# A vision tower's first attention: the order of its block steps inside a chunk, how its results are added, and the tokenizer's first steps

## Chip, cores and metric

The kernel runs on one core of a Trainium2 chip. The metric is device time in microseconds (us). The kernel before the change takes 2812.41 us, the median of three runs (2807.48 to 2813.47).

The core has five engines with a queue of instructions each, worked off in the order of issue: TensorE (PE; PEld are its weight loads), VectorE (DVE), ScalarE (ACT), GpSimd (POOL) and SyncE (SP, which issues DMAs). They meet through semaphores. SBUF is the core's working memory, PSUM the small memory into which TensorE writes.

## What is computed

128 images of 128x128 pass a tokenizer (two convolutions with batch norms, 64 tokens of 256 features an image), then two layers of attention and feed-forward. The change is in the tokenizer and in the first attention, which is this, over 64 tokens of an image, with 8 groups of 32 features:

```python
Q = x @ Wq.T; K = x @ Wk.T; V = x @ Wv.T          # x: layer norm of h
diff = Q.reshape(B, L, 1, G, Dg) - K.reshape(B, 1, L, G, Dg)
attn = einsum('bqkgd,d->bqkg', relu(diff), w_mlp) + b_mlp[0]
attn = softmax(relu(attn), axis=2)
out = einsum('bqkg,bkdg->bqdg', attn, V.reshape(B, L, Dg, G))
h = h + out.reshape(B, L, d_att)
```

The costly part is relu(q - k) for each query, key, image and feature. It is also max(q, k) - k, and the kernel uses both forms.

## The kernel before

All in float32; the running state h stays in SBUF as the tile `h2`, 128 partitions (2 images x 64 tokens) x 64 pairs of images x 256 features. The functions are called one after another: tokenizer, relu_attention, expert_attention, linear_attention, route, experts. The order of the work in the first two is written out by hand (`manual_schedule`): an engine's queue holds its instructions in the order in which the Python code issues them.

**Tokenizer** (L58 to L264). The image rows are loaded in 16 tiles `xt` of 512 KB, three in flight (`load`, L80); the first three, and all later ones, are issued by SP, the small weights `w1bd`, `bnv1`, `w`, `bnv2` by ACT's queue. `conv1(r)` (L123) is two matmuls, ACT writes one half (`ev`, L135), DVE the other (`h`, L132), and `differences(r)` (L139) makes two more on DVE. `between` (L146) makes `v`, on ACT, POOL or DVE. Five such rows precede the main loop, in which a `Unit` makes 72 matmuls (`products`, L177). In the preamble, at r == 2, stand the weights' negation (ACT, L229), the sum `w02` (POOL, L230) and the second batch norm's factors (`scale_offset`, L104 to L111: four small DVE instructions around a power on POOL, L108, and L233).

**First attention** (L267 to L719). 8 blocks of 16 images; a block has 8 chunks of 8 queries, so there are 64 chunks. A chunk makes 32 tiles of 128 x 8 queries x 64 keys, one for each pair of images' place i (0 to 15) and half of the features hf (0, 1), in three ways: `larger` (DVE, L486, max(q, k), four at a time straight from the queries in PSUM), `difference` (POOL subtracts, L494, ACT takes relu, L495, two at a time) and `by_query` (ACT, L504, four instructions for half a tile). `add(i0, hf)` sums four of them over the features with TensorE (`summed`, L301) into the scores `sc`, which `begin` (L481) has started with a correction `kb` for the max form. For the chunk before (`old`), `less_max` (DVE: L520, L521, L522), `exponents` (ACT, L527), `sums` (DVE, L530, L531), `weights` (POOL, L534), `transpose` (PE, L543) and `transposed` (ACT, L551) follow inside the current chunk. `queries` (PE, L422) and `queried` (ACT, L433) prepare the next one.

Between these, a table of work puts the steps of the neighbouring blocks at named places of a chunk: `at(n, place, step)` files a step under chunk n, and `do(n, place)` runs it there. Places O, A, B, C hold ACT's copies and normalisations; X, Y, Z hold PE's transposes, key, value and outcome products; V1 and V2 hold DVE's steps, W one of POOL's. In the order of PE's queue a chunk is: add(0,0), X, add(8,0), add(4,0), queries, Y, add(8,1), add(0,1), add(4,1), begin, transpose of the old, add(12,0), Z, add(12,1). For DVE: larger(0,0), larger(4,0), less_max, V1, larger(0,1), sums, larger(4,1), larger(12,1), V2. For ACT: relu of difference(8,0), O, half a by_query, relu of (10,0), exponents, half a by_query, relu of (8,1), A, relu of (10,1), queried, B, half a by_query, relu of (12,0), half a by_query, relu of (14,0), transposed, C.

A block's results come from `outcome` (PE, L443; two halves of the features), four copies `outcome_copied` (ACT, L454), transposes `back` (PE, L459) and `added` (DVE, L468), which adds 512 values a partition to `h2`. A result of half the features belongs to four of every eight neighbouring features, so `added` reads and writes `h2` with the feature index d outside in memory steps of 8 values (32 bytes). The PSUM tiles of all block steps come from one pool of three (`apq`). `first` (L565) prepares the first block ahead of the first chunk: statistics, normalisation, transposes, keys of both halves, queries, the correction.

## Time and profile before

| what | us |
|---|---|
| median of three runs | 2812.41 |
| the profiled execution | 2801.97 |
| its span, first to last instruction | 2800.3 |
| tokenizer, 0 to 180.7 | 180.7 |
| first attention up to its first search for a maximum, 180.7 to 218.1 | 37.4 |
| the chunks, 218.1 to 1118.2 | 900.1 |
| eight chunks of one block in the middle, 433.43 to 548.83 | 115.40 |

In those eight chunks the engines are busy so long: PE 112.86 us, DVE 106.13, ACT 99.84, POOL 100.12. The granted clock of TensorE is 1.00 throughout the chunks (0.97 over the tokenizer).

A row of the timeline gives the start, the length, the engine, the line, the operation, the tiles (written <- read), the shape, the count of instructions merged into the row, and in brackets the engine's idle time ahead of it and whose end stopped it. PE's rows overlap by the latency of the last matmul: 16 records of `summed` take 1.92 us, 24 take 2.78, so that one `add`, eight records, occupies PE for 0.86.

### The profile page before, as it was taken

The numbers are of one execution on the slowest core, as the hardware profiler recorded it, in microseconds if no ns is written. First come the engines' busy times: TensorE is split into PE (matmuls) and PEld (weight loads), VectorE is DVE, ScalarE is ACT, GpSimd is POOL, SyncE is SP. The second block draws the span as 40 slices with busy tenths as digits, with TensorE's granted clock in tenths as the row PEclk, the third lists the DMA queues.
The fourth block names the chain that finished last, engine by engine and source line by source line (L and its number), as shares of the span: only waits on it lengthen the run. The fifth ranks groups of instructions, "written<-read, shape, count | busy, mean of one in ns | idle before, by whom it ended". The sixth has DMA issues, their size and how long they took to land.

```text
span 2800.3 us, 76977 instructions
## 1 busy us (share of the span) xinstructions
PE 2608.5 (93%) x33260; PEld 1750.3 (63%) x33260; DVE 2041.6 (73%) x3046; ACT 1611.9 (58%) x3348; POOL 1633.1 (58%) x1412
## 2 busy tenths in 40 slices
PE   7989999999999998799999999999899964999997
PEld 3554444444444443688888888887466644888886
DVE  6759899998999998577778777776467766344443
ACT  3228888888888887456666566665354430233332
POOL 3328988888888888666565665643133211454444
PEclk9999999999999999799999999999899975999998
DMA  3000000000000000000000000000444432455554
GB/s 106 31 12 1 2 1 2 1 2 2 1 2 1 2 2 2 12 11 18 11 18 11 11 18 11 18 11 15 116 91 110 97 87 105 163 194 193 194 195 132
DMA packets 138064, 140.81 MB, mean 50 GB/s; under 512 B 107923, under 2 KB 121509, under 8 KB 130032
## 3 DMA queue, kind: packets, MB, share of 16 engines
q1 hardware_dynamic: 126640, 118.40, 14.1%
q0 software_dynamic: 7648, 14.77, 1.6%
q8 instruction: 263, 4.31, 0.6%
q10 hardware_dynamic: 3424, 2.60, 0.3%
q14 instruction: 89, 0.73, 0.1%
HBM read 103.93 MB, written 32.54 MB: 49 GB/s over the span
## 4 chain that ended last, share of the span: by engine, by line
PE 81%; DVE 10%; ACT 3%; issue 3%; POOL 1%; DMA 1%; ACTq 0%; SPq 0%; DVEq 0%; POOLq 0%
PE sc L301 13%; PE ph L1714 6%; PE po L1730 6%; PE pqk L894 6%; PE pv L906 5%; PE pz L975 5%; PE pc L177 4%; PE pt L962 4%; PE sc L926 4%; DVE m L486 3%; PE pq L1174 3%; PE po L989 2%; PE pt L543 2%; PE sc L481 2%; PE pv L387 2%
## 5 line engine op out<-in xcount | busy, mean ns | idle before, releaser
L494 POOL TENSOR_TENSOR m<-q,k 128x1024 f32<-128x1024 f32 x384 | 719.7, 1905 | 34.0 <-PE sc L301 11.5
L486 DVE TENSOR_TENSOR m<-pc,k 128x2048 f32<-128x2048 f32 (+1 forms) x320 | 643.7, 2058 | 0.0
L301 PE MATMUL sc<-m,wide 128*32 128x512 f32 x4096 | 533.8, 599 | 23.5 <-DVE m L486 17.7
L495 ACT ACTIVATE m<-m 128x1024 f32<-128x1024 f32 x384 | 402.1, 1049 | 17.1 <-POOL m L494 17.1
L301 PEld LDWEIGHTS sc<-m,wide 128*32 128x32 f32 x4096 | 128.1, 109 | 272.0 <-issue 132.8
L504 ACT ACTIVATE m<-k,q 128x64 f32<-128x64 f32 x1024 | 270.3, 337 | 0.9 <-DVE k L380 0.9
L938 DVE TENSOR_REDUCE mx<-sc 128x16 f32<-128x1024 f32 x128 | 156.1, 1220 | 155.0 <-PE sc L926 129.8
L953 POOL TENSOR_TENSOR e<-e,mx 128x1024 f32<-128x1024 f32 x128 | 243.7, 1904 | 10.1 <-POOL mx L952 0.2
L898 ACT COPY qk<-pqk 128x512 f32<-128x512 f32 x256 | 138.8, 604 | 132.6 <-PE pqk L894 132.6
L952 POOL TENSOR_TENSOR mx<-mx,gate 128x16 f32<-128x16 f32 x128 | 27.8, 217 | 312.8 <-ACT z L983 146.8
L1714 PE MATMUL ph<-xt,w1s 128*128 128x256 f32 x896 | 201.0, 383 | 1.3 <-DVE xt L1705 0.8
L1730 PE MATMUL po<-w2s,hT 128*128 128x256 f32 x896 | 198.0, 379 | 0.0
L965 ACT COPY pT<-pt 128x512 f32<-128x512 f32 x256 | 138.9, 599 | 99.3 <-PE pt L962 98.7
L1714 PEld LDWEIGHTS ph<-xt,w1s 128*128 128x128 f32 x896 | 171.9, 192 | 26.0 <-DVE xt L1705 1.2
L1718 ACT ACTIVATE hT<-ph,w1s 128x256 f32<-128x256 f32 x224 | 93.4, 471 | 155.5 <-PE ph L1714 82.3
L1730 PEld LDWEIGHTS po<-w2s,hT 128*128 128x128 f32 x896 | 168.1, 190 | 21.7
L894 PE MATMUL pqk<-xT,w 64*128 64x128 f32 x2048 | 169.4, 289 | 2.6 <-issue 2.4
L939 DVE TENSOR_TENSOR e<-sc,mx 128x1024 f32<-128x1024 f32 x128 | 156.8, 1225 | 4.4
L1748 POOL DMA_INDIRECT out<-y,rout x56 | 56.8, 1014 | 172.6 <-ACT hT L1718 124.8
L894 PEld LDWEIGHTS pqk<-xT,w 64*128 64x128 f32 x2048 | 142.5, 189 | 20.3 <-issue 11.6
L945 DVE TENSOR_REDUCE mx<-e 128x16 f32<-128x1024 f32 x128 | 153.2, 1197 | 1.2 <-ACT e L942 1.0
L962 PE MATMUL pt<-ident,e 128*128 128x128 f32 x1024 | 144.4, 282 | 4.5 <-POOL e L953 1.2
(292 smaller groups left out, 4974.8 us busy)
## 6 DMA issues: line engine op xcount, KB each, us to landing
w1s<-in_we SPq DMA_DIRECT2D x30, 1028.0 KB
w2s<-in_we SPq DMA_DIRECT2D x30, 1024.0 KB
xt<-in_x SPq DMA_DIRECT2D x16, 512.0 KB
hd<-h SPq DMA_DIRECT2D x16, 512.0 KB
x<-hd SPq DMA_DIRECT2D x16, 512.0 KB
h<-hd SPq DMA_DIRECT2D x4, 2048.0 KB
hx<-h SPq DMA_DIRECT2D x4, 2048.0 KB
out<-h SPq DMA_DIRECT2D x4, 2048.0 KB
```

What stands on the lines that cost most here:

```text
L301: nc.tensor.matmul(dst[j : j + 32], wide[:, hf, s : s + 32], part, start=start, stop=stop)
L486: nc.vector.tensor_tensor(m, bcast(self.pq[:, hf, i : i + n], 3, T), k, ALU.max)
L494: nc.gpsimd.tensor_tensor(m, bcast(self.q[:, hf, s : s + 2], 3, T), k, ALU.subtract)
L495: nc.scalar.activation(m, m, AF.Relu)
L504: nc.scalar.activation(self.parts[i, hf][:, q], self.blk.k[:, hf, i], AF.Relu, bias=self.q[:, hf, i - NB // 2, q : q + 1], scale=-1.0,)
L894: nc.tensor.matmul(pq[par][:, k, eh, :], w[r, f : f + P], self.xT[r, fc], start=True, stop=True)
L938: nc.vector.tensor_reduce(mx, sc, AX.X, ALU.max)
L939: nc.vector.tensor_sub(e, sc, bcast(mx, 2, T))
L953: nc.gpsimd.tensor_mul(e, e, bcast(sm, 2, T))
L962: nc.tensor.transpose(pt[:, cq, :], e[:, i : i + 2, :].rearrange("p e s -> p (e s)"), c.ident)
L1714: nc.tensor.matmul(ph[:, j], self.w1[:, w0 : w0 + P], self.xt[:, fc], start=(fc == 0), stop=(fc == 1))
L1730: nc.tensor.matmul(po, self.hT[:, f, r * P : r * P + P], self.w2[:, f, :], start=(f == 0), stop=(f == 7))
```

## The change

It has five parts.

1. Tokenizer: the small first weights go to SP's queue, ahead of SP's loads; row tile 0 goes to ACT's queue. The weights' negation and the sum `w02` move from r == 2 to r == 1; the second batch norm's factors move from r == 2 to behind the last `between` of the preamble.
2. `first` is cut: the keys of the second half of the features, their copies (both now on DVE), the sums and the correction run inside chunk 0, behind its first difference and its first `larger`; so does `begin` of chunk 0.
3. In a chunk PE's queue becomes: add(0,0), add(8,0), add(4,0), X, queries, add(8,1), add(0,1), add(4,1), begin, transpose of the old, Z, add(12,0), add(12,1). Place Y is gone; Z stands ahead of V2, add(12,0) and `transposed`.
4. The block steps are filed under other chunks and places. Counted 0 to 7 within a block of chunks, PE's steps (for the next block, and for the results of the block before) are now: 0: X and Z, a transpose each; 1: X and Z, one half of the outcome each; 2: Z a transpose; 3: X two `back`, Z a transpose; 4: X two `back`, Z keys; 5: X keys, keys, Z keys; 6: X values, Z key sums and values; 7: X values, values. `added` stands in V1 of chunks 3 and 4 (before: 2 and 3), the statistics of the block after next in V2 of chunks 3 and 4 (before: 4 and 5).
5. `back(i)` transposes both halves of two pairs, and `added(i)` adds 2 pairs x 256 whole features: `h2` is read and written without gaps, the PSUM tile is read in steps of 32 values. It is called four times a block, 512 values a partition each, as before.

```diff
@@ -77,19 +77,19 @@
     ):
         rows = {}
 
-        def load(r):
+        def load(r, eng=nc.sync):
             rows[r] = xt = xp.tile([P, 8, B], F32, tag="xt", name="xt")
-            nc.sync.dma_start(xt, x[r])
+            eng.dma_start(xt, x[r])
 
 
         w1bd = wp.tile([P, P], F32, name="w1bd")
         nc.vector.memset(w1bd, 0.0)
         bnv1 = wp.tile([P, 4], F32, name="bnv1")
         bnv2 = wp.tile([P, 4, 4], F32, name="bnv2")
-        load(0)
         for k in range(2):
-            nc.scalar.dma_start(w1bd[k * 64 : (k + 1) * 64, k * 64 : (k + 1) * 64], w1)
-            nc.scalar.dma_start(bnv1[k * 64 : (k + 1) * 64, :], bn1)
+            nc.sync.dma_start(w1bd[k * 64 : (k + 1) * 64, k * 64 : (k + 1) * 64], w1)
+            nc.sync.dma_start(bnv1[k * 64 : (k + 1) * 64, :], bn1)
+        load(0, nc.scalar)
         for r in range(1, 3):
             load(r)
 
@@ -223,16 +223,16 @@
                     nc.gpsimd.tensor_add(w[:, :, 1], w[:, :, 0], w[:, :, 2])
                 differences(r)
                 if r == 1:
+                    nc.scalar.mul(w[:, :, 2], w[:, :, 2], -1.0)
+                    nc.gpsimd.tensor_add(w02, w[:, 0:2], w[:, 2:4])
                     between(0, 0, 0)
                 elif r == 2:
                     between(0, 0, 1)
-                    nc.scalar.mul(w[:, :, 2], w[:, :, 2], -1.0)
-                    nc.gpsimd.tensor_add(w02, w[:, 0:2], w[:, 2:4])
-                    s2, o2 = scale_offset(lambda i: bnv2[:, i, :], [P, 4], "2")
-                    n2 = wp.tile([P, 4], F32, name="n2")
-                    nc.vector.tensor_scalar_mul(n2, s2, -1.0)
             for k in range(2):
                 between(0, 2, k)
+            s2, o2 = scale_offset(lambda i: bnv2[:, i, :], [P, 4], "2")
+            n2 = wp.tile([P, 4], F32, name="n2")
+            nc.vector.tensor_scalar_mul(n2, s2, -1.0)
             for m in range(4):
                 for ab in range(4):
                     u = Unit(m, ab)
@@ -453,19 +453,22 @@
                     self.oT = np_.tile([P, 2, NP, 2, T], F32, tag="oT", name="oT", bufs=1)
                 nc.scalar.copy(self.oT[:, hf, :, par], self.ps["o", hf][par])
 
-            def back(self, hf, i):
-                self.ps["h", hf, i] = pt = psq.tile([P, 4, P], F32, tag="pq", name="pto")
-                for n in range(4):
-                    nc.tensor.transpose(
-                        pt[:, n], self.oT[:, hf, 4 * i + n].rearrange("p b t -> p (b t)"), c.ident
-                    )
-
-            def added(self, hf, i):
-
-                p0 = self.p0 + 4 * i
-                hv = h2[:, p0 : p0 + 4].rearrange("p n (d g) -> p n g d", g=8)[:, :, hf * 4 : hf * 4 + 4]
-                pt = self.ps.pop(("h", hf, i))
-                nc.vector.tensor_add(hv, hv, pt.rearrange("p n (g d) -> p n g d", d=32))
+            def back(self, i):
+
+                self.ps["h", i] = pt = psq.tile([P, 2, D], F32, tag="pq", name="pto")
+                for n in range(2):
+                    for hf in range(2):
+                        nc.tensor.transpose(
+                            pt[:, n, hf * P : hf * P + P],
+                            self.oT[:, hf, 2 * i + n].rearrange("p b t -> p (b t)"),
+                            c.ident,
+                        )
+
+            def added(self, i):
+
+                hv = h2[:, self.p0 + 2 * i : self.p0 + 2 * i + 2].rearrange("p n (d g) -> p n d g", g=8)
+                pt = self.ps.pop(("h", i))
+                nc.vector.tensor_add(hv, hv, pt.rearrange("p n (g d) -> p n d g", d=32))
 
         class Chunk:
 
@@ -576,9 +579,11 @@
                 x.keyed(s, 0, s == 1)
             x.queries(0)
             x.queried(0)
+
+        def first_rest(x):
             for s in range(2):
                 x.keys(s, 1)
-                x.keyed(s, 1, s == 1)
+                x.keyed(s, 1, True)
             x.key_sums()
             x.correction()
 
@@ -588,60 +593,61 @@
             at(n + 9, "X", of(x.outcome, 0))
             at(n + 9, "A", of(x.outcome_copied, 0, 0))
             at(n + 9, "B", of(x.outcome_copied, 0, 1))
-            at(n + 9, "Y", of(x.outcome, 1))
+            at(n + 9, "Z", of(x.outcome, 1))
             at(n + 9, "C", of(x.outcome_copied, 1, 0))
-            at(n + 9, "Z", of(x.back, 0, 0))
             at(n + 10, "O", of(x.outcome_copied, 1, 1))
-            at(n + 10, "X", of(x.back, 0, 1))
-            at(n + 10, "V1", of(x.added, 0, 0), of(x.added, 0, 1))
-            at(n + 10, "Z", of(x.back, 1, 0))
-            at(n + 11, "X", of(x.back, 1, 1))
-            at(n + 11, "V1", of(x.added, 1, 0), of(x.added, 1, 1))
+            for i in range(4):
+                at(n + 11 + i // 2, "X", of(x.back, i))
+                at(n + 11 + i // 2, "V1", of(x.added, i))
             if b == 0:
-                for i, (m, pe, act) in enumerate(((0, "X", "A"), (1, "X", "A"), (2, "X", "A"), (2, "Y", "B"))):
-                    at(m, pe, of(x.values, i))
-                    at(m, act, of(x.valued, i))
+                for i in range(4):
+                    at(i, "X", of(x.values, i))
+                    at(i, "A", of(x.valued, i))
                 continue
 
             if b == 1:
                 at(0, "V1", of(x.statistics, 0), of(x.statistics, 1))
                 at(0, "W", x.factors)
                 at(0, "C", of(x.normal, 0), of(x.normal, 1))
-                at(1, "A", of(x.normal, 2))
-                at(1, "B", of(x.normal, 3), of(x.normal, 4))
+                at(1, "A", of(x.normal, 2), of(x.normal, 3))
+                at(1, "X", of(x.transpose, 0))
+                at(1, "B", of(x.transposed, 0))
+                at(1, "Z", of(x.transpose, 1))
+                at(1, "C", of(x.normal, 4))
             else:
-                at(n - 12, "V2", of(x.statistics, 0))
-                at(n - 11, "V2", of(x.statistics, 1))
-                at(n - 10, "W", x.factors)
-                at(n - 9, "B", of(x.normal, 0), of(x.normal, 1))
-                at(n - 8, "A", of(x.normal, 2))
-                at(n - 8, "B", of(x.normal, 3), of(x.normal, 4))
-            at(n - 8, "Z", of(x.transpose, 0))
-            at(n - 7, "O", of(x.transposed, 0))
+                at(n - 13, "V2", of(x.statistics, 0))
+                at(n - 12, "V2", of(x.statistics, 1))
+                at(n - 11, "W", x.factors)
+                at(n - 11, "C", of(x.normal, 0))
+                at(n - 10, "B", of(x.normal, 1))
+                at(n - 9, "C", of(x.normal, 2))
+                at(n - 8, "X", of(x.transpose, 0))
+                at(n - 8, "A", of(x.transposed, 0))
+                at(n - 8, "B", of(x.normal, 3))
+                at(n - 8, "Z", of(x.transpose, 1))
+                at(n - 8, "C", of(x.normal, 4))
+            at(n - 7 if b > 1 else n - 6, "O", of(x.transposed, 1))
             at(n - 6, "A", of(x.normal, 5))
-            at(n - 6, "B", of(x.normal, 6), of(x.normal, 7))
-            at(n - 5, "X", of(x.transpose, 1))
-            at(n - 5, "A", of(x.transposed, 1))
-            at(n - 5, "Y", of(x.keys, 0, 0))
-            at(n - 5, "B", of(x.keyed, 0, 0))
-            at(n - 5, "Z", of(x.transpose, 2))
-            at(n - 4, "O", of(x.transposed, 2))
-            at(n - 4, "X", of(x.transpose, 3), of(x.keys, 0, 1))
-            at(n - 4, "A", of(x.transposed, 3))
-            at(n - 4, "B", of(x.keyed, 0, 1))
-            at(n - 4, "Z", of(x.values, 0))
-            at(n - 3, "O", of(x.valued, 0))
-            at(n - 3, "X", of(x.keys, 1, 0))
-            at(n - 3, "A", of(x.keyed, 1, 0))
-            at(n - 3, "Z", of(x.values, 1))
-            at(n - 2, "O", of(x.valued, 1))
-            at(n - 2, "X", of(x.keys, 1, 1))
-            at(n - 2, "A", of(x.keyed, 1, 1))
-            at(n - 2, "Z", x.key_sums)
+            at(n - 6, "Z", of(x.transpose, 2))
+            at(n - 6, "C", of(x.normal, 6))
+            at(n - 5, "O", of(x.transposed, 2))
+            at(n - 5, "A", of(x.normal, 7))
+            at(n - 5, "Z", of(x.transpose, 3))
+            at(n - 4, "O", of(x.transposed, 3))
+            at(n - 4, "Z", of(x.keys, 0, 0))
+            at(n - 4, "C", of(x.keyed, 0, 0))
+            at(n - 3, "X", of(x.keys, 0, 1), of(x.keys, 1, 0))
+            at(n - 3, "A", of(x.keyed, 0, 1))
+            at(n - 3, "B", of(x.keyed, 1, 0))
+            at(n - 3, "Z", of(x.keys, 1, 1))
+            at(n - 2, "O", of(x.keyed, 1, 1))
+            at(n - 2, "X", of(x.values, 0))
+            at(n - 2, "A", of(x.valued, 0))
+            at(n - 2, "Z", x.key_sums, of(x.values, 1))
+            at(n - 2, "C", of(x.valued, 1))
             at(n - 1, "V1", x.correction)
-            at(n - 1, "X", of(x.values, 2))
+            at(n - 1, "X", of(x.values, 2), of(x.values, 3))
             at(n - 1, "A", of(x.valued, 2))
-            at(n - 1, "Y", of(x.values, 3))
             at(n - 1, "B", of(x.valued, 3))
 
         def do(n, place):
@@ -652,29 +658,30 @@
             seq = [(x, q0) for x in blocks for q0 in range(0, T, 8)]
             first(blocks[0])
             ch, old = Chunk(*seq[0]), None
-            ch.begin()
             for n in range(len(seq)):
                 new = None
                 ch.difference(8, 0)
                 ch.larger(mvp, 0, 4, 0)
                 do(n, "O")
+                if n == 0:
+                    first_rest(blocks[0])
+                    ch.begin()
                 ch.by_query(14, 1, 0)
                 ch.add(0, 0)
+                ch.difference(10, 0)
+                ch.larger(mvp, 4, 4, 0)
+                ch.add(8, 0)
+                ch.add(4, 0)
                 do(n, "X")
-                ch.difference(10, 0)
-                ch.add(8, 0)
-                ch.larger(mvp, 4, 4, 0)
-                ch.add(4, 0)
+                if n + 1 < len(seq):
+                    seq[n + 1][0].queries(seq[n + 1][1])
                 if old:
                     old.less_max()
                     old.exponents()
                 ch.by_query(14, 1, 1)
-                if n + 1 < len(seq):
-                    seq[n + 1][0].queries(seq[n + 1][1])
                 ch.difference(8, 1)
                 do(n, "A")
                 do(n, "V1")
-                do(n, "Y")
                 ch.difference(10, 1)
                 if n + 1 < len(seq):
                     seq[n + 1][0].queried(seq[n + 1][1])
@@ -697,6 +704,7 @@
                     new.begin()
                 if old:
                     old.transpose()
+                do(n, "Z")
                 ch.larger(mgp, 12, 2, 1)
                 do(n, "V2")
                 ch.difference(14, 0)
@@ -704,7 +712,6 @@
                     old.transposed()
                 do(n, "C")
                 ch.add(12, 0)
-                do(n, "Z")
                 ch.add(12, 1, True)
                 old, ch = ch, new
             old.less_max()
@@ -714,7 +721,7 @@
             old.transpose()
             old.transposed()
             for n in range(len(seq), len(seq) + 12):
-                for place in ("O", "X", "A", "V1", "Y", "B", "V2", "C", "Z"):
+                for place in ("O", "X", "A", "V1", "B", "Z", "V2", "C"):
                     do(n, place)
         assert not work
 
```

## The prediction

> **What bounds the kernel now.** I read the page first: the busy shares and the chain that ended last.
>
> ```profile
> PE 2608.5 (93%) x33260; PEld 1750.3 (63%) x33260; DVE 2041.6 (73%) x3046; ACT 1611.9 (58%) x3348; POOL 1633.1 (58%) x1412
> ...
> PE 81%; DVE 10%; ACT 3%; issue 3%; POOL 1%; DMA 1%; ACTq 0%; SPq 0%; DVEq 0%; POOLq 0%
> ```
>
> TensorE carries the chain. The change takes no matmul away (16 transposes of results a block before and after), so it can only change how long PE waits. For that I cut one block into its eight chunks, at each chunk's first add:
>
> ```profile
> core 0: us, PE busy (x) PEld busy (x) DVE busy (x) ACT busy (x) POOL busy (x), PEclk, DMA share, GB/s
> 433.43:447.08 13.65, 12.88 (x116) 4.90 (x111) 12.24 (x10) 13.05 (x31) 12.67 (x8) 1.00 0.01 2
> ...
> 461.13:475.99 14.86, 13.54 (x121) 5.16 (x117) 14.28 (x12) 13.39 (x33) 12.01 (x8) 1.00 0.00 1
> ...
> sum 115.40, PE 112.86 PEld 49.30 DVE 106.13 ACT 99.84 POOL 100.12; mean PE 14.11 PEld 6.16 DVE 13.27 ACT 12.48 POOL 12.52
> ```
>
> PE looks full, but a matmul row counts its latency as busy. By starts, a chunk without waits is 8 adds of 0.86, queries 1.05, begin 1.06, transposes 1.08 and 0.4 of switching: 10.45 us. A block adds values 4 x 1.92, keys 4 x 1.85, transposes 8 x 0.6, outcomes 2 x 1.45, key sums 0.85: 23.65. So 8 x 10.45 + 23.65 = 107.25 us, and 8.15 of the 115.40 are waits. Two kinds make them. First ScalarE's, in the timeline of chunk 0:
>
> ```profile
> 430.17 1.15 PE L543 MATMUL pt<-ident,e 128*64 128x64 f32 x32
> ...
> 431.79 0.57 ACT L551 COPY at<-pt 128x512 f32<-128x512 f32 x1
> 432.26 1.06 ACT L495 ACTIVATE m<-m 128x1024 f32<-128x1024 f32 x1
> 433.21 1.06 ACT L504 ACTIVATE m<-k,q 128x64 f32<-128x64 f32 x4
> 434.17 1.04 ACT L495 ACTIVATE m<-m 128x1024 f32<-128x1024 f32 x1
> 435.27 1.91 PE L301 MATMUL sc<-m,wide 128*32 128x512 f32 x12 [0.39 <-ACT m L495]
> ```
>
> Between PE's weight transposes and the second half of add(8,0) ScalarE does four things in order; the add waits. With PE work in place X ahead of it the wait is covered, as in chunks 4 to 6. Second VectorE's, where it adds results (chunk 3):
>
> ```profile
> 360.85 0.70 DVE L520 TENSOR_REDUCE pc<-sc 128x8 f32<-128x512 f32 x1 [0.40 <-PE sc L301]
> 361.54 0.66 PE L459 MATMUL pto<-ident,oT 128*128 128x128 f32 x4
> ...
> 362.46 2.17 DVE L468 TENSOR_TENSOR h<-h,pto 128x512 f32<-128x512 f32 x2
> ...
> 364.55 2.27 DVE L486 TENSOR_TENSOR m<-pc,k 128x2048 f32<-128x2048 f32 x1
> ...
> 369.86 1.07 PE L301 MATMUL sc<-m,wide 128*32 128x512 f32 x8 [0.39 <-DVE m L486]
> ```
>
> The two adds push both following `larger`, and add(4,1) waits. Today they start directly behind less_max (its last instruction, L522, ran from 361.85 to 362.54): their transposes are through.
>
> **Part 1, tokenizer.** PE starts densely at 33.55:
>
> ```profile
> 21.06 3.51 POOL L230 TENSOR_TENSOR w<-w 128x1536 f32<-128x1536 f32 x1 [8.12 <-ACT w L229]
> 21.32 4.86 DVE L154 TENSOR_TENSOR v<-h 128x1536 f32<-128x1536 f32 x1
> ...
> 27.95 0.81 DVE L132 TENSOR_SCALAR h<-pa,s,o 128x512 f32<-128x512 f32 x1
> 28.81 4.81 PE L130 MATMUL pa<-xt,w1bd 128*128 128x512 f32 x6 [4.10 <-DVE h L132]
> 33.55 2.81 PE L177 MATMUL pc<-v,w 128*64 128x256 f32 x24
> ```
>
> DVE's L154 took 1.76 at 34.84; here, beside POOL's sum, 4.86. Moved up, the sum runs from about 16.4 (ACT's negation takes the gap behind its second row, 15.3 to 16.4) to 19.9 and no longer covers L154: -3.1. The factors (26.10 to 27.95) go behind the preamble: -1.85. L132 of row 3 then starts near 23.1, and row 4's matmul follows its twin (24.7); rows 4 and 5 and their copies take to 27 to 29. I take -5.7 at 33.55, bounds -3 (the clock row is half here; it may stay so) and -7. [...] The swapped queues: the second w1bd issue stays at about 2.06 and landed 5.7 later beside three row tiles; now it has one tile and 1 MB of `w` beside it. I take 0, bounds -2 and +1. SP's tiles 1 and 2 are now issued behind four small DMAs of 0.6, some 2 us later, and are wanted at 12.55 and 15.32; that is hidden unless they land 5 us later than today. The factors' new waits (POOL behind one L154, then 1.0) hold DVE to about 34, while PE reaches the next unit only near 37: nothing.
>
> **Part 2, chunk 0.** DVE's first `larger` starts at about 194.9, not 199.6, and two key copies (0.69) come between; so DVE is 2.1 ahead, begin finds no wait (1.07), and chunk 0 ends 2.6 earlier. Bounds -1 and -3.5.
>
> **Part 5, whole rows.** L468 takes 1.12 (median); its nearest row for the new form, L204 (same size, strided PSUM in, SBUF without gaps out), 0.69. I take 0.70 (bounds 0.6 to 1.5): -1.7 of DVE a block. [...]
>
> **Parts 3 and 4, the chunk.** Here X moves behind add(8,0) and add(4,0). Chunk 3, walked from its first add = 0. ScalarE: the weight transposes end 2.4 earlier (Z 0.7, two adds 1.72); then L551 0.5, C 0.55, relu 0.96, O 0.57, by_query 0.96, relu 1.0, i.e. 4.54: the relu ends at 2.15. Add(8,0) ends at 2.15 + 0.06 + 0.86 = 3.07 in place of 1.72: 1.35 lost, no X in front to cover it. Add(4,0) ends at 3.93, the two `back` at 4.6 and 5.15. less_max is done at 1.86, but the first row add waits for its transposes: 4.7 to 5.4, the second to 6.1. Then larger 2.25, sums 0.83, larger 2.25 with latencies: 11.4; add(4,1) ends 0.92 later, at 12.3, where PE alone would be at 8.85: 3.4 lost. Behind add(4,1): begin to transposes 2.25, Z 0.7, two adds 1.72: 17.0 us. DVE still has larger 1.13, the moved statistics 2.1 and two larger 4.4: done at 19.0, so less_max of chunk 4 starts 1.75 late, which its own wait for transposes hides (row adds done at 5.5, chunk 17.6).
>
> So behind a waiting row add stand both other `larger` and the sums on DVE, and for these wait add(0,1), add(4,1) and, through POOL's weights, the next transposes.
>
> The same walk for the other chunks, each with its own steps in C, O, X, A and Z. The second wait that ScalarE makes is at add(8,1): its relu (10,1) ends at about 5.5 (today 5.95 with one step in A, both behind exponents, by_query and relu (8,1)) plus what A holds or waits for. Before, after, and PE's own work after in brackets:
>
> | chunk | before | after | why |
> |---|---|---|---|
> | 0 | 13.65 | 13.6 (11.65) | relu at 2.25: 1.45; add(8,1) 0.5 |
> | 1 | 14.05 | 15.2 (13.35) | relu 2.1 behind C and O: 1.3; A copies an outcome that X makes late: 0.55 |
> | 2 | 14.86 | 14.2 (11.05) | `transposed` waits for the second outcome in Z, relu at 2.9: 2.1; add(8,1) 1.05 |
> | 3 | 14.89 | 17.0 (12.25) | above |
> | 4 | 14.87 | 17.6 (13.5) | relu 1.55: 0.75; row adds 3.35 |
> | 5 | 14.66 | 17.0 (16.0) | C copies keys that Z ends late, relu 1.8: 1.0 |
> | 6 | 13.84 | 15.7 (15.15) | A copies values that X makes late: 0.55 |
> | 7 | 14.58 | 15.15 (14.3) | C copies values, relu 1.8: 0.85 |
>
> Sum 115.4 before, 125.4 after: waits of 18.2 in place of 8.15, +10 a block (bounds: +2, rival a, and +13, with 0.4 more at each relu). POOL's (10,0) ends before the chunk's start in most chunks today and stays covered; if not, relu waits for it as long.
>
> **The sum.** Six full blocks +60. Block 0 (no results yet, chunks 1 to 7): relu waits of 0.9 to 1.7 a chunk, +5.5. Block 7 (no next block): chunks 3 and 4 wait as above, 1.6 + 3.7, chunk 1 +1.2, chunk 2 -1.8: +4.7. Chunk 0 -2.6, tokenizer -5.7; the end, where the same steps follow each other, 0. Together +62: 2802 becomes 2864 for the profiled execution, which lies 10.4 under the median of the runs; on the median 2812.4 it gives **2874 us**.
>
> **Rivals.** (a) Only VectorE waits: ScalarE is ready in time, because Z now stands between the weight transposes and the last adds. For it: relu ended at 1.07 in chunk 3 today. Against: C and O add 1.1, and 0.8 is needed. Row adds then end at 4.75, chunks 3 and 4 wait 3.4 and 3.7, chunk 2 1.7, chunk 0 1.1: 9.9, +1.75 a block. Six blocks +10.5, block 0 +3, block 7 +4, start -8.3: +9, so 2821. (b) Faster: the block's waits shrink. If the transposes of X were done by the end of less_max (1.86) and the relu by 0.8, chunks 3 and 4 would wait 1.9 each, 2 and 0 1.7 and 1.1: 6.6, -1.5 in each of seven blocks, -10.5 - 8.3 = -19: 2794. Decided by X's place: three adds end at 2.58 at the earliest; so it is unlikely. The sign turns where a block loses under 8.3 / 7 = 1.2 more than now. (c) The whole-row adds are not cheaper: 1.1 to 1.5 each, +0.8 to +1.6 in each of two chunks of seven blocks, +11 to +22: 2885 to 2896. (d) It all cancels: 2812.
>
> **Chances.** Forecast 0.60 (2845 to 2890), (a) 0.20, (b) 0.09, (c) 0.08, (d) 0.03. Range 2816 to 2896: from (a), with 5 for the start's bounds, to (c). 0.2% (5.6 us) is what a measurement of this kernel can tell from none: faster 0.09, same 0.03, slower 0.88.
>
> **What would show it.** Chunks 3 and 4 of a block at 17 to 18 us; row adds of 0.7 that start 0.5 to 3 us behind L522, waiting for `pto`; L301 waiting for ACT in most chunks; a block near 125; PE's first L177 near 28; chunk 0 ending 2 to 3 us earlier against the tokenizer's end. I am wrong if add(8,0) does not wait for relu, or if row adds start as soon as less_max is done.

## The result and the profile after

The changed kernel takes **2876.93 us** (median of 4 runs, 2873.92 to 2880.66); the kernel before took 2809.94 in the runs beside it (4 runs, 2806.90 to 2813.47). The ratio is 1.0239, 95% interval 1.0219 to 1.0258: slower by 67 us. The profiled execution took 2877.26 us with a span of 2875.4, 75.1 above the span of before.

The page after, busy shares and chain:

```profile
PE 2650.5 (92%) x33260; PEld 1764.1 (61%) x33260; DVE 2028.3 (71%) x3047; ACT 1608.7 (56%) x3347; POOL 1632.6 (57%) x1412
...
PE 49%; DVE 3%; issue 2%; ACT 2%; POOL 1%; DMA 1%; SPq 0%; POOLq 0%; ACTq 0%; DVEq 0%
```

The matmuls are the same 33260. VectorE does 13 us less (2041.6 before), and still the kernel is longer. The chain's shares add up to 58% and the lines it names all belong to later stages: it was not followed back into the first attention, so the waits there are read from the other views. Block 2 cut into its chunks (columns as before the change):

```profile
core 0: us, PE busy (x) PEld busy (x) DVE busy (x) ACT busy (x) POOL busy (x), PEclk, DMA share, GB/s
445.28:458.93 13.65, 13.18 (x118) 5.35 (x114) 12.23 (x10) 12.94 (x30) 12.25 (x8) 1.00 0.01 2
...
488.36:505.13 16.77, 13.32 (x122) 5.28 (x118) 13.37 (x20) 12.45 (x30) 12.25 (x8) 1.00 0.01 1
505.13:522.74 17.61, 15.23 (x122) 5.83 (x122) 16.73 (x21) 11.48 (x27) 12.25 (x8) 1.00 0.01 1
...
sum 124.60, PE 116.83 PEld 50.60 DVE 104.46 ACT 99.57 POOL 100.28; mean PE 14.60 PEld 6.32 DVE 13.06 ACT 12.45 POOL 12.53
```

The block takes 124.6 in place of 115.4; chunks 3 and 4 carry most of it, with fewer busy microseconds on VectorE over the block (104.5 for 106.1). The timeline of chunks 0 and 3 of this block shows both waits:

```profile
446.54 1.04 ACT L498 ACTIVATE m<-m 128x1024 f32<-128x1024 f32 x1
447.64 1.91 PE L301 MATMUL sc<-m,wide 128*32 128x512 f32 x12 [0.47 <-ACT m L498]
...
489.64 0.69 DVE L525 SCALAR_TENSOR_TENSOR e<-sc,mx 128x512 f32<-128x512 f32 x1
490.61 1.91 PE L301 MATMUL sc<-m,wide 128*32 128x512 f32 x12 [0.37 <-ACT m L498]
492.45 1.09 PE L461 MATMUL pto<-ident,oT 128*128 128x128 f32 x8
493.14 1.28 DVE L471 TENSOR_TENSOR h<-h,pto 128x512 f32<-128x512 f32 x2 [2.82 <-PE pto L461]
494.35 2.29 DVE L489 TENSOR_TENSOR m<-pc,k 128x2048 f32<-128x2048 f32 x1
496.69 1.07 PE L301 MATMUL sc<-m,wide 128*32 128x512 f32 x8 [1.17 <-DVE m L489]
499.67 0.64 PE L301 MATMUL sc<-m,wide 128*32 128x512 f32 x4 [1.92 <-DVE m L489]
```

First TensorE waits for ScalarE's relu at the adds of the first half, so the transposes behind them (492.45) come late. VectorE is done with less_max at 490.3 and then stands 2.82 us before the row adds. The next `larger` (494.35) is queued behind them, and add(0,1) and add(4,1) wait 1.17 and 1.92 us for it and for the one after it. The sums over the first attention (us in all, times, longest) say the same; first before, then after:

```profile
PEld sc L301 <- DVE m L486: 45.1, 62, 2.7
PEld sc L301 <- ACT m L495: 44.1, 54, 1.9
PE sc L301 <- DVE m L486: 16.6, 16, 1.8
```

```profile
PEld sc L301 <- ACT m L498: 96.2, 108, 1.9
PEld sc L301 <- DVE m L489: 81.4, 65, 2.8
PE sc L301 <- DVE m L489: 43.0, 28, 1.9
DVE h L471 <- PE pto L461: 33.5, 14, 2.8
```

The adds now wait for ScalarE's relus twice as long and as often, and twice as long for VectorE. The last line, the row adds' wait of 2.4 us in each of 14 chunks, is new.

**What the prediction did not have** is in the clock. Block 2 is the only full block with full clock throughout; in block 1 the same two chunks read:

```profile
359.44:377.82 18.38, 14.93 (x125) 5.63 (x121) 15.00 (x20) 12.45 (x30) 12.24 (x8) 0.91 0.00 1
377.82:398.16 20.34, 17.31 (x125) 6.80 (x121) 15.88 (x21) 11.59 (x27) 12.24 (x8) 0.83 0.00 1
```

Their granted clock is 0.91 and 0.83, and they take 38.7 us in place of 34.4. The clock halves once or twice, for 3.41 or 6.83 us each time, in these chunks of five of the six full blocks, and of block 7. In the kernel before it stayed at 1.0 through all chunks.

The tokenizer's start after:

```profile
16.27 0.69 DVE L142 TENSOR_TENSOR h<-h,ev 128x512 f32<-128x512 f32 x1
16.58 3.67 POOL L227 TENSOR_TENSOR w<-w 128x1536 f32<-128x1536 f32 x1 [3.68 <-ACT w L226]
...
21.49 1.76 DVE L154 TENSOR_TENSOR v<-h 128x1536 f32<-128x1536 f32 x1
...
27.60 2.81 PE L177 MATMUL pc<-v,w 128*64 128x256 f32 x24
```

POOL's sum no longer lies beside L154, which takes 1.76 in place of 4.86, and L177 starts at 27.60 in place of 33.55. That VectorE's L142 began 0.31 us ahead of POOL's L227 turns out to matter.

### The profile page after: what moved, and what is told of

Read it like the earlier page. It is cut to its first block, busy times and chain, and to the rows that moved or that the text cites. A ratio compares the mean times of both kernels' runs of the same rounds, so it can differ in the third digit from the quotient of the medians.

```text
span 2875.4 us, 76966 instructions
## 1 busy us (share of the span) xinstructions
PE 2650.5 (92%) x33260; PEld 1764.1 (61%) x33260; DVE 2028.3 (71%) x3047; ACT 1608.7 (56%) x3347; POOL 1632.6 (57%) x1412
## 3 DMA queue, kind: packets, MB, share of 16 engines
q1 hardware_dynamic: 126816, 117.91, 13.7%
## 4 chain that ended last, share of the span: by engine, by line
PE 49%; DVE 3%; issue 2%; ACT 2%; POOL 1%; DMA 1%; SPq 0%; POOLq 0%; ACTq 0%; DVEq 0%
PE ph L1721 6%; PE po L1737 6%; PE pqk L901 6%; PE pv L913 5%; PE pz L982 4%; PE pt L969 4%; PE sc L933 3%; PE pq L1181 3%; PE po L996 2%; PE pv L1195 2%; PE po L1296 1%; PE pg L853 1%; PE pi L1602 1%; PE po L997 1%; DVE sth L1312 1%
## 5 line engine op out<-in xcount | busy, mean ns | idle before, releaser
L301 PE MATMUL sc<-m,wide 128*32 128x512 f32 x4096 | 566.8, 606 | 60.9 <-DVE m L489 43.2
L301 PEld LDWEIGHTS sc<-m,wide 128*32 128x32 f32 x4096 | 134.1, 109 | 397.0 <-issue 196.2
```

Source lines behind the costliest of these rows:

```text
L301: nc.tensor.matmul(dst[j : j + 32], wide[:, hf, s : s + 32], part, start=start, stop=stop)
```

## The experiments

Times are medians. The kernel before, run beside them, had 2807.0 beside the first four experiments, 2805.4 beside the next four, and 2806.7 and 2805.1 beside the last two pairs; in the result above it had 2809.9. The theory: the place of X makes the row adds wait for their transposes, and behind them TensorE waits for VectorE; the two long waits drop the clock on top. The main rival: what costs is VectorE's amount of work in chunks 3 and 4 (row adds and statistics together).

**Part 1 alone** on the kernel before, its three hunks; the core of them:

```
                 if r == 1:
+                    nc.scalar.mul(w[:, :, 2], w[:, :, 2], -1.0)
+                    nc.gpsimd.tensor_add(w02, w[:, 0:2], w[:, 2:4])
                     between(0, 0, 0)
...
             for k in range(2):
                 between(0, 2, k)
+            s2, o2 = scale_offset(lambda i: bnv2[:, i, :], [P, 4], "2")
```

> The kernel before with part 1 alone (the first loads on the other queues, the products of the filters ahead, the scales of the second normalization behind). Theory: the start is a step of its own; TensorE's dense run of L177 begins near 27.6 in place of 33.55 and nothing behind it gives that back: -6 us, 2804 by the median of before (bounds 2801 to 2807), and the eight blocks keep 115.4 each. Rival (the gain is lost behind it, because the first chunks wait for something else): within 2 us of the kernel before.

2802.47 (12 runs), ratio 0.9984 (0.9974 to 0.9993): -4.6 us. In the profile the first add comes 5.1 earlier (196.8 for 201.9) and blocks 1 to 5 keep 115.4 to 115.6, but at the last add only 1.2 is left: block 0 takes 2.2 and block 7 1.6 more, each with a stretch of half clock that the kernel before doesn't have. The same kernel with the sum on VectorE (below) has neither and keeps 6.2 of its 6.2. The medians say that the gain is kept; what dropped the clock in this one profile was not tried.

**X early**, in the changed kernel:

```
                 ch.add(0, 0)
+                do(n, "X")
                 ch.difference(10, 0)
                 ch.larger(mvp, 4, 4, 0)
                 ch.add(8, 0)
                 ch.add(4, 0)
-                do(n, "X")
```

> The changed kernel with one edit: place X (the transposes of the outcome, the values) stands again between add(0,0) and add(8,0), where the kernel before had it. Theory (VectorE's row adds wait for transposes that stand behind add(8,0) and add(4,0)): the row adds start right behind less_max without a wait, chunks 3 and 4 together fall from 37.5 to about 31, a block from 127.4 to 114 or 115, the clock stays 1.0 within the chunks; 2803 (2795 to 2815). Rival (what costs is the amount of VectorE work in those two chunks, row adds and statistics together, wherever the transposes stand): 2850 or more, chunks 3 and 4 above 35 together.

2811.85 (10 runs), ratio 1.0016 (1.0005 to 1.0027): one moved line takes back 65 of the 67 us by these medians (62 with each kernel laid against the kernel before beside it). From the first add to the last the profiles differ by 73 us (995.0 and 922.0); the rest is the start, which is 6.2 later here for a reason told further down, and the end. Chunks 3 and 4 together take 30.8, the clock stays 1.0. The same chunk 3, with row adds that stand directly behind less_max:

```profile
478.25 0.70 DVE L523 TENSOR_REDUCE pc<-sc 128x8 f32<-128x512 f32 x1 [1.47 <-PE sc L301]
479.25 0.69 DVE L525 SCALAR_TENSOR_TENSOR e<-sc,mx 128x512 f32<-128x512 f32 x1
479.86 1.27 DVE L471 TENSOR_TENSOR h<-h,pto 128x512 f32<-128x512 f32 x2
481.05 2.29 DVE L489 TENSOR_TENSOR m<-pc,k 128x2048 f32<-128x2048 f32 x1
```

VectorE has the same instructions here, so the rival of the amount falls. The block takes 117.5, though, not 114 to 115, and the time is 9 above my number; what is left is parted below, in the two runs with whole rows in the old order and the one with later statistics.

**Row adds in V2**, in the changed kernel (X stays late):

```
-                at(n + 11 + i // 2, "V1", of(x.added, i))
+                at(n + 11 + i // 2, "V2", of(x.added, i))
```

> The changed kernel with the row adds in place V2 (behind the adds of the second half) in place of V1; the transposes stay where the change put them. Theory (it is the wait of the row adds, ahead of the maxima of the second half, that delays add(0,1) and add(4,1)): no wait of the row adds for a transpose is left, chunks 3 and 4 together near 30 or 31, a block near 119 to 121, no half clock within the chunks; about 2827 (2815 to 2840). Rival (amount of work of VectorE in those chunks): within 8 us of the changed kernel, 2869 to 2885.

2827.51 (4 runs), as expected to the microsecond. No row add waits, chunks 3 and 4 take 29.7, the clock stays 1.0. So of the 65 us that X costs, 49 come by way of the row adds' wait, and 16 are the other waits, for ScalarE above all (in the profiles, from the first add to the last, 57 and 16 of the 73). The waits of the weight loads here:

```profile
PEld sc L301 <- ACT m L498: 105.9, 120, 1.9
PEld sc L301 <- DVE m L489: 35.0, 68, 2.0
```

With X early they are 69.3 for ScalarE and 47.8 for VectorE.

**Redundant matmuls** in the waits of chunks 3 and 4, in the changed kernel:

```
+                warm = n > 8 and n % 8 in (3, 4)
+                if warm:
+                    new.fill()
                 ch.larger(mvp, 0, 4, 1)
                 ch.add(0, 1)
+                if warm:
+                    new.fill()
...
+            def fill(self):
...
+                nc.tensor.matmul(self.sc, c.ident, bcast(self.blk.kb, 1, 8), start=True, stop=True)
...
```

> The changed kernel with two redundant matmuls (1.12 us each) in chunks 3 and 4 of a block, ahead of add(0,1) and of add(4,1), where TensorE waits 1.17 and 1.92 us for VectorE's maxima; their result is overwritten. Theory (the two long waits within one stretch of 3.4 us drop the granted clock, and the half clock then costs 1 to 2 us a chunk): the clock stays 1.0 within chunks 3 and 4, the two together take 34.4 to 34.8 in every block in place of 37.5 on average, and the kernel gets 13 to 20 us faster, about 2860. Rival (the half clock falls into waits and costs nothing, or the redundant matmuls push back what follows): 2874 or more.

2867.18 (5 runs): -9.7, less than expected, but with more work on TensorE. The windows of block 1:

```profile
366.67:383.44 16.77, 15.43 (x126) 5.87 (x121) 13.37 (x20) 12.45 (x30) 12.24 (x8) 1.00 0.00 1
383.44:401.62 18.18, 17.42 (x127) 6.32 (x127) 17.30 (x21) 11.49 (x27) 12.26 (x8) 1.00 0.00 1
```

The clock is 1.0 and the two chunks take 35.0 for 38.7. Over blocks 1 to 7 the two profiles differ by 18.7 us; this kernel's own profile loses 7.3 of it at the start (first add at 203.1 for 195.9), by what is shown below. So the half clock is no symptom: it costs some 2.7 us a block, net of what the redundant matmuls cost (0.6 in block 1, 35.0 against the 34.4 of the changed kernel's block 2).

**Half rows**, in the changed kernel (`back` and `added` themselves as before the change, same places):

```
-                at(n + 11 + i // 2, "X", of(x.back, i))
-                at(n + 11 + i // 2, "V1", of(x.added, i))
+                at(n + 11 + i // 2, "X", of(x.back, i // 2, i % 2))
+                at(n + 11 + i // 2, "V1", of(x.added, i // 2, i % 2))
```

> The changed kernel with the transposes and row adds by half rows of before (four of 1.1 us a block in place of four of 0.68), everything else as changed. Theory (in chunks 3 and 4 the row adds stand in VectorE's way between the late transposes and the maxima that TensorE waits for, so their length counts in full): each of the two chunks 0.8 us longer, a block +1.7, over seven blocks +12, so 2889 (2881 to 2900), a little more if the half clock grows with it. Rival (the length of a row add is hidden in the wait for the transposes): 2877, within 3 us of the changed kernel.

2902.36 (4 runs): +25, twice what was expected. The row adds take 1.1 again, chunks 3 and 4 rise from 37.5 to 40.2 on average over blocks 1 to 6, and the clock now halves in all seven blocks, for 10.2 us each (13.7 in the first; in the changed kernel 6.8 to 10.2 in six of them). The sign of the theory holds, its size doesn't: with the longer row add came more half clock, and this profile's start was 7.5 later.

**X late**, in the kernel before:

```
                 ch.add(0, 0)
-                do(n, "X")
                 ch.difference(10, 0)
                 ch.add(8, 0)
                 ch.larger(mvp, 4, 4, 0)
                 ch.add(4, 0)
+                do(n, "X")
```

> The kernel before with one edit: place X stands behind add(4,0) in place of ahead of add(8,0); row adds, statistics and all other steps as before. From the pair of runs above: with the row adds out of the way, moving X cost 2828 - 2812 = 16 us, some 2.2 us a block. Theory: here one of the two transposes that a chunk's row adds need stands in X and is late by some 0.5 us only, so the wait of the row adds is small, and what remains is the relu wait at add(8,0): +1.5 to +3 a block, 2818 to 2832, and no half clock within the chunks. Rival (X late by itself already makes the row adds' wait, whatever else moves): +6 a block or more, 2850 or above. Rival (X late costs nothing without the other moves): within 5 us of before.

2858.51 (4 runs), ratio 1.0200 (1.0180 to 1.0221): +53. My theory was wrong here and the first rival right: X late makes the loss by itself. Chunk 2 of block 1:

```profile
355.09 1.91 PE L301 MATMUL sc<-m,wide 128*32 128x512 f32 x12 [0.23 <-ACT m L495]
...
357.62 1.10 DVE L468 TENSOR_TENSOR h<-h,pto 128x512 f32<-128x512 f32 x1 [1.63 <-PE pto L459]
358.63 2.27 DVE L486 TENSOR_TENSOR m<-pc,k 128x2048 f32<-128x2048 f32 x1
...
360.96 1.07 PE L301 MATMUL sc<-m,wide 128*32 128x512 f32 x8 [0.90 <-DVE m L486]
...
363.94 1.94 PE L301 MATMUL sc<-m,wide 128*32 128x512 f32 x8 [1.92 <-DVE m L486]
```

I had put the wait of the row add at 0.5 us. It is 1.15 on average over 14 chunks (up to 1.63), because add(8,0) waits for the relu first (its weight load for 1.13 in this chunk) and pushes the transposes back. It is the same chain as in the changed kernel, the half clock included (in blocks 1, 3, 5 and 7). And other chunks lose as well: chunk 1 is 1.9 us longer (outcomes in X), chunk 5 1.2 (keys).

**Whole rows in the old order** (the kernel before with part 1 and part 5; transposes in Z and X as before, one a chunk later); the new filing of the steps:

```
...
+            at(n + 10, "X", of(x.back, 0))
+            at(n + 10, "V1", of(x.added, 0))
+            at(n + 10, "Z", of(x.back, 1))
+            at(n + 11, "X", of(x.back, 2))
+            at(n + 11, "V1", of(x.added, 1), of(x.added, 2))
+            at(n + 11, "Z", of(x.back, 3))
+            at(n + 12, "V1", of(x.added, 3))
```

> The kernel before with part 1 and with whole row adds, in the chunk order of before (transposes in Z and X, row adds in V1 behind them, the last one a chunk later). Theory (VectorE's time in chunks 2 and 3 is what TensorE waits for there, 1.32 and 0.44 us a block in the profile of before): the shorter row adds take 1.0 to 1.7 us a block out of it, so 7 to 11 us below the run with part 1 alone (2802.5): 2793 (2790 to 2798). Rival (VectorE's time there is slack that TensorE's own work covers): 2800 to 2805.

2790.79 (6 runs), ratio 0.9942 (0.9925 to 0.9960). Against part 1 alone -11.7, a block 113.9 for 115.4. Part 5 is a gain. Whole rows need both halves of the outcome, so one transpose and one row add also stand a chunk later here; the two were not parted in this order, but the half rows above, at unchanged places, have the same sign.

**The same with part 2**, the core of it:

```
...
+                if n == 0:
+                    first_rest(blocks[0])
+                    ch.begin()
                 ch.by_query(14, 1, 0)
...
```

> As the run with whole rows in the old order, with part 2 as well (the second half's keys of block 0 and the correction behind the first operations of chunk 0). Theory: chunk 0 ends 1 to 2.6 us earlier, so 1 to 2.6 us below that run, about 2791. Rival (the first chunk's maxima and keys contend for VectorE and ScalarE and nothing is gained): the same within 1 us. Together with the run with X early (2811.9) this tells part 3 (the placements of statistics, normal, transposes, keys and values): what is left between the two, some 20 us, is its price.

2791.93 (5 runs). In the profile the first chunk is 1.05 shorter (14.27 for 15.32); the medians don't show it, within their scatter of some 10 us.

**Statistics later**, in the kernel with X early (chunks 4 and 5 again):

```
-                at(n - 13, "V2", of(x.statistics, 0))
-                at(n - 12, "V2", of(x.statistics, 1))
-                at(n - 11, "W", x.factors)
-                at(n - 11, "C", of(x.normal, 0))
-                at(n - 10, "B", of(x.normal, 1))
+                at(n - 12, "V2", of(x.statistics, 0))
+                at(n - 11, "V2", of(x.statistics, 1))
+                at(n - 10, "W", x.factors)
+                at(n - 10, "C", of(x.normal, 0))
+                at(n - 9, "B", of(x.normal, 1))
```

> The run with X early (2811.9, 20 us above the kernel with whole rows in the old order) with one edit more: the statistics of the next block a chunk later again (chunks 4 and 5 in place of 3 and 4, as before the change), with the factors and the first three normalizations one place or one chunk later. Theory (what is left of part 3's price is VectorE's queue in chunks 3 and 4, which holds row adds and statistics together: TensorE waits 2.3 us in chunk 4): chunk 4 falls from 16.95 to about 15, a block by some 2 us, 2798 (2794 to 2804). Rival (it is TensorE's own matmuls, keys and transposes heaped in chunks 5 and 6, 16.05 and 15.21 us without a wait, while others fall short): within 4 us, 2808 to 2814, chunks 5 and 6 as they are.

2804.28 (12 runs): -7.6. Chunk 4 falls from 16.95 to 15.19, as the theory has it; chunks 5 and 6 stay at 16.05 and 15.21, as the rival has it. The expectations call part 3 what the description of the change calls part 4 (the filing of the block steps), together with the moves of Y and Z in part 3. Of the 20 us of these placements (2811.9 against 2791.9) some 8 are statistics beside row adds. The rest may come from TensorE's matmuls heaped in chunks 5 and 6, where it has no gap, while in chunk 2 it waits 0.97; that split was not tried.

**The sum of the filters on VectorE**, three times: on the kernel with whole rows and part 2, on part 1 alone, and on the changed kernel.

```
-                    nc.gpsimd.tensor_add(w02, w[:, 0:2], w[:, 2:4])
+                    nc.vector.tensor_add(w02, w[:, 0:2], w[:, 2:4])
```

> As the run with whole rows, old order and part 2 (2791.9), with one edit: the sum of the filters that part 1 put ahead (L227) on VectorE in place of GpSimd. In six of eight profiles with part 1, VectorE's L142 took 3.91 us in place of 0.69 because GpSimd's L227 (3.7 to 3.9 us) had begun just ahead of it, and TensorE's dense run of L177 began at 34.5 to 35.5 us; in the other two L142 began first and L177 stood at 27.4 and 27.6. Theory (that meeting of the two engines decides the start): with no GpSimd operation there, L142 takes 0.7 us in every profile, L177 begins at 28 to 30, and the median falls by 3 to 6 us: 2786 to 2789. Rival (the late start has another source, the half clock of the first 12 us, and L142's time is covered): L177 at 33 or later, 2790 to 2794; the sum's 1.76 us on VectorE could even add to it.

> The kernel before with part 1 alone (2802.5) and the sum of the filters (L227) on VectorE in place of GpSimd. In the profiles so far the full clock came at 10.5 to 12.3 us or at 15.5 to 16.9 us of the span, and with part 1 every late clock went with the late L177 (34.5 to 35.5). Theory (the late clock costs so much only because it brings VectorE's L142 behind GpSimd's L227): 2796 to 2800, and if this profile has the late clock, L142 takes 0.7 us and L177 begins at 31 or earlier. Rival (the late clock by itself makes the late start): 2801 to 2805, and with a late clock L177 at 33 or later.

> The changed kernel with the same edit (L227 on VectorE). Theory: 3 to 6 us below the changed kernel, 2871 to 2874, with less spread between its runs, the blocks as in the changed kernel (124.6 to 128.6); with a late clock L177 at 31 or earlier. Rival: 2875 to 2880, L177 at 33 or later where the clock is late.

What raised the question is the start of the kernel with X early, whose tokenizer is that of the changed kernel:

```profile
17.14 3.90 POOL L227 TENSOR_TENSOR w<-w 128x1536 f32<-128x1536 f32 x1 [4.88 <-ACT w L226]
17.68 3.91 DVE L142 TENSOR_TENSOR h<-h,ev 128x512 f32<-128x512 f32 x1
...
21.62 1.48 ACT L151 ACTIVATE v<-h 128x1536 f32<-128x1536 f32 x1 [4.56 <-DVE h L142]
...
34.81 1.52 PE L177 MATMUL pc<-v,w 128*64 128x256 f32 x12
```

L142 began 0.54 us behind L227, ended 0.55 behind its end (21.59 and 21.04), and L177 stands at 34.8. The full clock had come late (16.9 us; 12.3 in the profile of the changed kernel), which made TensorE's second row late (with the third it ends at 18.41 for 17.45). With the sum on VectorE, the changed kernel's profile had a late clock too (17.2), and reads:

```profile
17.65 0.69 DVE L142 TENSOR_TENSOR h<-h,ev 128x512 f32<-128x512 f32 x1
18.25 1.75 DVE L227 TENSOR_TENSOR w<-w 128x1536 f32<-128x1536 f32 x1
...
29.28 2.81 PE L177 MATMUL pc<-v,w 128*64 128x256 f32 x24
```

So in the one profile that shows it a late clock without the meeting puts L177 at 29.3, some 2.8 behind the 26.5 of an early one (part 1 alone with this edit), and the meeting with GpSimd costs the other 5. (The profiles of the other two had an early clock, 10.5 and 10.8 us, with L177 at 26.3 and 26.5, and can't tell.) The medians: 2785.44 (5 runs, 2783.4 to 2788.9) against 2791.9, and 2798.64 (12 runs) against 2802.5, at or just below what the theory gave. Neither gain is clear of the scatter, though: the ratios to the kernel before are 0.9931 (0.9912 to 0.9950) against 0.9945 (0.9929 to 0.9961), and 0.9978 (0.9969 to 0.9988) against 0.9984 (0.9974 to 0.9993), 7.8 and 1.8 us. What is shown is the start in the profiles. The changed kernel has 2878.20 (5 runs) against 2876.9: by its median this is the rival's number, though its L177 is the theory's. Its clock halved in all six full blocks of this profile, which would hide a gain of 3; that is not settled.

The first of these, parts 1, 2 and 5 in the old order with the sum on VectorE, is the fastest of the study and **beats both kernels**: ratio 0.9931 to the kernel before (0.9912 to 0.9950).

The medians, strung together so that each line has one part more:

| kernel | us | step |
|---|---|---|
| before | 2807.0 | |
| + part 1 | 2802.5 | -4.6 |
| + part 5, whole rows | 2790.8 | -11.7 |
| + part 2 | 2791.9 | +1.1 |
| + part 4 and Y, Z of part 3, placements | 2811.9 | +20.0 |
| + X behind the adds, of part 3 (the changed kernel) | 2876.9 | +65.1 |

Each laid against the kernel before beside it, the lines stand at -4.6, -14.7, -13.5, +4.8 and +67.0, which makes the last two steps 18 and 62. I take a step as sure to some 5 us, since the runs of one kernel scatter by 7 to 12. Part 2's step is none by that.

## Why the prediction was right

The time was foreseen (2874), and for the reason given; the table of the chunks can be laid beside the one block whose clock was undisturbed, and beside the mean of blocks 1 to 6:

| chunk | predicted | block 2 | mean |
|---|---|---|---|
| 0 | 13.6 | 13.65 | 13.65 |
| 1 | 15.2 | 15.55 | 15.25 |
| 2 | 14.2 | 13.88 | 13.85 |
| 3 | 17.0 | 16.77 | 18.50 |
| 4 | 17.6 | 17.61 | 19.03 |
| 5 | 17.0 | 16.73 | 16.73 |
| 6 | 15.7 | 15.57 | 15.57 |
| 7 | 15.15 | 14.83 | 14.83 |
| sum | 125.4 | 124.6 | 127.4 |

- **TensorE bounds, no matmul is taken away**: right; only waits of the adds grew.
- **Parts 3 and 4**: right in mechanism and, without the clock, in size. X early and row adds in V2 show the chain link by link. The gap is the clock, a term the sum did not have: chunks 3 and 4 take 37.5 on average for 34.4. With +73 for six blocks the profile is 13 above the predicted 60; by the undisturbed block it would have been 55.
- **Part 5**: 0.70 predicted, 0.68 measured (median of 32). L142, as many values between SBUF tiles, has the same median, so the strided read from PSUM shows no cost here. Rival (c) falls: no run shows the 1.1 to 1.5 that it gives the new row add (0.68 to 0.69 in all 32).
- **Part 1**: -5.7 predicted, -5.95 in the profile of the changed kernel, -4.6 by the medians of part 1 alone (its profile kept 1.2 of 5.1). The step that was wrong is that the moved sum "no longer covers L154" and so covers nothing: it comes within 0.5 us of L142, and in six of the nine profiles with part 1's sum on GpSimd it held L142 for 3.9 us.
- **Part 2**: -2.6 predicted; chunk 0 itself went from 15.32 to 13.54, -1.8 (-1.9 against the tokenizer's end, where the prediction named 2 to 3 as its sign), and -1.05 with part 2 in the old order. Mis-sized, within its bounds.
- **Block 0's other chunks** +6.7 (predicted 5.5), **block 7** +6.7 (4.7, its clock halved too), **the end** -3.4 (0): behind the last add the kernels of this study, which have the same code there, take 1684 to 1689 us, so this is within their scatter.
- **Rival (a)** fell because the relu waits are there (96 us for 44 in the waits of the weight loads). **(b)** and **(d)** fell with it.

The closeness of the hit is luck. The profiled execution was forecast at 2864 and took 2877.3, 13 more: the missing clock (+17 over six blocks) and the smaller gains were offset only in part by blocks a little shorter than predicted (-5) and by the end. The median came within 3 us because the prediction then added 10.4, by which the profiled execution of before lay under its median; the changed kernel's lies at its median (2877.26 and 2876.93).

## What to carry to other kernels

Before you move a producer behind other work on a saturated engine, list what waits for it in the queues of the other engines, and what is queued behind each of these waiting instructions: here one line in TensorE's order cost some 65 us, three quarters of it by way of 0.7 us row adds. A step that is cheaper (whole rows, -11.7) and a schedule that is worse can come in one change; string them apart before judging either. And price a new wait of about 2 us on TensorE with the clock that it may cost behind it (here some 2.7 us a block).

## What the runs showed of the hardware

**The clock fell behind partial idleness.** The half-clock rows in the chunks start on a grid of 3.41 us. I summed, in each stretch of that grid at full clock between the first add and the last, the time without a matmul. In the changed kernel, the one with half rows, X late in the kernel before, and the changed kernel with the sum on VectorE, half clock followed 43 stretches, all with 1.92 to 2.35 us of such time; no other stretch of the chunks had more than 1.92 (two had that, the next 1.83). With the redundant matmuls none had over 1.13, and none fell. The limit is not sharp: with part 1 alone half clock followed two stretches, of 1.93 and 1.78. In the changed kernel half clock followed a stretch with a single gap of 1.92 (up to 1007.78 us), and one with two gaps of 1.1 (up to 385.64, and from 386.70 on).

**Two operations 0.5 us apart.** L142 took 0.69 us when it began 0.31 ahead of GpSimd's L227, and 3.91 when it began 0.54 behind it. Begun second, L142 ended 0.55 behind L227's end, and L154 of before 1.61 behind the end of L230 (26.18 and 24.57), near the 0.69 and 1.76 that they take alone: as if VectorE's operation got going only when GpSimd's was through. That GpSimd waits when it begins second, these rows don't show: L227 took 3.67 then, and 3.90 when it began first.
